# A decoder layer on one core: turns of attention weights placed only behind steps with products, and tokens sent to one expert a slot

## The chip, the cores and the metric

The kernel runs on one core of a Trainium2 chip. The metric is the device time of one execution in microseconds (us). The kernel before takes 1240.89 us, the median of 14 runs that lie between 1239.35 and 1242.22. The engines are named PE (TensorE, matrix products and transposes), DVE (VectorE), ACT (ScalarE), POOL (GpSimd) and SP (SyncE). Here POOL issues all indirect DMAs, which gather or scatter rows by a list of indices, and SP issues the plain ones.

## The reference

One layer on 32 batches of 112 tokens of width 256, all in 32-bit floats: self-attention of 16 heads with a causal window of 64, cross-attention of 16 heads on 375 context rows a batch with a relative bias, and a mixture of 8 experts (width 512), of which each token uses two. Cut to what matters:

```python
x = x + self_attention(layernorm(x))            # 16 heads, window 64
x = x + cross_attention(layernorm(x), context)  # 16 heads, 375 keys, bias by distance
xf = layernorm(x).reshape(3584, 256)
probs = softmax(xf @ router_w.T)                # 8 experts
probs = (probs * top2_mask) ; probs /= probs.sum(-1) + 1e-9
h = silu(xf @ gate_w[e] + gate_b[e]) * (xf @ up_w[e] + up_b[e])
x = x + sum over the two experts e of probs[e] * (h @ down_w[e] + down_b[e])
```

## The kernel before, in words

**Groups and slots.** The 32 batches form 8 groups (0 to 7) of 4 batches. The program is unrolled into *slots*. Group g owns the 16 slots from `base[g]` = 20 + 16g on; a slot takes a quarter of the cross-attention heads of one batch of that group, and a quarter of the self-attention heads of a batch two groups ahead. In slot s, `scores` (L464 ff.) lets PE make the raw scores (L477 cross, L488 self), DVE add bias or mask and take the row's minimum (L503), and POOL subtract that minimum from the whole tile (L509). Two slots later `weigh` turns the same tile: four PE transposes (L530) of up to 125 columns put one *turn* into a PSUM buffer, and one ACT activation (L531) empties it through exp. The pool of these PSUM buffers, `ps_tr`, has two. A slot with both kinds of scores has four turns (three of the cross scores, one, the *self turn*, of the self scores). `average` (L554) then multiplies the turned weights by the values; `divide` (L568 to L574, the last of them POOL's product into `by_q`), `turn` (L584, DVE) and `attended` (L597 on PE, L602 on DVE) finish a batch.

**Order.** The bodies of PE, DVE and ACT are issued exactly in the order in which the Python code calls them (`IN_ORDER`). The loop at the end of the program (L1266 ff.) does in each slot: the scores, the averages, the first two turns, then the list `steps[slot]` of other work with one of the remaining turns after each step, then whatever turns are left, then the list `late[slot]`, and a part of the planning or of the experts' tiles. Steps are put into the slots by hand with `put` and `put_late`: projections of keys and values for the coming batch (`cross_k`, L384; `cross_v`, L450), layer norms (`norm`, L344 to L353; `scale`, L364, which makes the tile `xn`; `norm_t`, L378, its transposes), the router, loads, and `blank`, which fills one of 28 parts of the DRAM table `xslots` with zeros and issues only a DMA on SP. POOL's instructions are put into the order of the program too (`queue_pool`); members of a *loose* group, such as "sent", may pass each other.

**Routing.** The functions of one route of a group are `logits` (L615), `choose` (L626 to L634), `rank` (L641 to L651, with POOL's product into `pr` at L643), `front`, `gate`, `weight_gates`, `count` and `address` (L718), each a slot after the one before. Then `send` writes each token's normalised row, its number and its gates (265 words) into two rows of `xslots`, one for each of its two experts (k = 0 and 1): an indirect DMA by POOL for each batch and each k (L725), eight for a group. The route of group g is sent in the slots after `base[g+1]`. The row tile of the third layer norm has the tag `xr`.

**Experts.** The experts work on tiles of up to 256 rows that have the same expert. `fetch_weights` (L960) gathers one expert's weights into the tile `w`, `fetch_rows` (L973) gathers two times 128 rows from `xslots` into `xg`; both are indirect DMAs on POOL. Tiles 0 and 1 are fetched while group 7 is still in attention, at `base[7]` + 5 to + 8. `experts` starts at `base[8]` + 5 and fetches tiles 2 and on, three tiles ahead. A tile is turned on PE (L1015, `xtp`), copied by DVE (L1020, `xT`), multiplied (L1030, `gu`), passed through silu on ACT (L1035) and DVE (L1038, `hid`), multiplied again (L1049, `py`), scaled by its gate on ACT (L1055, `y`) and added to the output in DRAM by an indirect DMA of POOL (L1056). For every `which == 0` tile, `fetch_rows` is told to follow the first 48 sends.

Of the kernel before, what the change touches and what calls it, by code (L numbers as in the profile page):

```python
# [11 lines left out]
F32 = mybir.dt.float32  # L12
# [7 lines left out]
B, S, D = 32, 112, 256  # L20
# [6 lines left out]
GB = 4  # L27
NG = B // GB
# [51 lines left out]
def decoder_kernel(  # L80
# [41 lines left out]
    def pool_order():  # L122


        traced = nc.cur_bb.bb.instructions
        mark, before_these, these, group = traced[-1], [], [], None

        def queue():
            nonlocal mark, before_these, these, group
            k = len(traced)  # L130
            while traced[k - 1] is not mark:
                k -= 1
            mark = traced[-1]
            for ins in traced[k:]:
                if ins.engine != mybir.EngineType.Pool:
                    continue
                own = loose.get(ins.name)
                if own is None or own != group:
                    before_these, these, group = these or before_these, [], own
                these.append(ins)  # L140
                for other in before_these:
                    tc.add_manual_dep(
                        ins, other.name,
                        mybir.DependencyInfo(
                            mybir.DependencyClass.NoSync, mybir.DependencyReason.DATA
                        ),
                        reason="order",
                    )

        return queue  # L150
# [25 lines left out]
    with ExitStack() as att, ExitStack() as own_att:  # L176
# [179 lines left out]
        def scale(g, n, b2):  # L356
            if b2 == 0:
                tag, width = ("xr", ROW) if n == 3 else ("xn", D)
                pool = keep if n == 3 else selfp
                xn = pool.tile([S, GB, width], F32, tag=tag, name=f"xn{g}_{n}")  # L360
                normed[g, n] = xn, *normed[g, n]
            xn, rstd, shift = normed[g, n]
            for b in (2 * b2, 2 * b2 + 1):
                nc.scalar.activation(  # L364
                    xn[:, b, :D], xs[g][:, b, :], AF.Identity,
                    bias=shift[:, b:b + 1], scale=rstd[:, b:b + 1],
                )
            if b2 == 1:
                normed[g, n] = [xn]
# [348 lines left out]
            nc.vector.tensor_copy(to, at)  # L718
            rows_of[g] = to

        def send(g, b):

            to, xn = rows_of[g], normed[g, 3][0]
            for k in range(2):
                sent = nc.gpsimd.indirect_dma_start(  # L725
                    out=xslots, out_offset=bass.IndirectOffsetOnAxis(
                        ap=to[:, k, b:b + 1], axis=0),
                    in_=xn[:, b, :], in_offset=None,
                )

                tc.declare_no_dep(sent.ins, group="sent", reason="rows differ")
                tc.add_to_no_dep_group("sent", sent.ins)
                all_sent.append(sent.ins)
                loose[sent.ins.name] = "sent"
# [343 lines left out]
        def experts():  # L1078


            fetch(2)
            pending, xT = None, begun[2]
            for k in range(body):
                if k + 3 <= body:
                    fetch(k + 3)
                if k:
                    hid = hidden_of(k)
                    for f in range(NFC):
                        hidden(k, xT, hid, f)
                        if f == 1:  # L1090
                            yield
                else:
                    hid = begun[1]
                    yield
                to, gate = target(k)
                yield
                if k:
                    xT = turned_in(k + 1)
                if pending is not None:
                    down(*pending)  # L1100
                pending = (k, hid, to, gate)
                if k == body - NTAIL:
                    left_over["n"] = nc.values_load(
                        in_tail[0:1, 0:1], min_val=0, max_val=NTAIL,
                        skip_runtime_bounds_check_because="at most so many are left",
                    )
            down(*pending)
            left_over["xT"] = xT
# [24 lines left out]
        def put(slot, fn, *args):  # L1133
            steps.setdefault(slot, []).append(partial(fn, *args))
# [4 lines left out]
        def put_late(slot, fn, *args):  # L1139
            late.setdefault(slot, []).append(partial(fn, *args))  # L1140

        def put_norm(norm_at, norm_t_at, g, n, scale_at=None):
            for c in range(NC2):
                put_late(norm_at - 2 + c, norm, g, n, c)
                put(scale_at or norm_at + 1, scale, g, n, c)
                put(norm_t_at, norm_t, g, n, c)
# [13 lines left out]
        def put_route(g, norm_at, norm_t_at):  # L1160
            put_norm(norm_at, norm_t_at, g, 3)
            put(norm_t_at + 1, logits, g)
            for i, fn in enumerate((choose, rank, front, gate, weight_gates, count, address)):
                put_late(norm_t_at + 1 + i, fn, g)
            for b in range(GB):
                put(norm_t_at + 8 + b, send, g, b)
            turn_at = 8 if g == NG - 2 else 7
            put(norm_t_at + turn_at, turn_gates, g)
            put(norm_t_at + (9 if g == NG - 1 else 10), down_bias, g)
# [60 lines left out]
        for g in range(NG):  # L1230
# [9 lines left out]
            if g >= NX:  # L1240
                put(base[g - NX + 1] + 22, load_x, g)
        put_route(NG - 1, base[NG] + 5, base[NG] + 8)
        free_self, free_all = base[NG - 1], base[NG] + 5
        plan_at = {base[EARLY + 1] - 1: first_plan, base[NG] + 14: later_plan}
# [9 lines left out]
        put(base[NG] + 4, begin_next)  # L1254
        put_late(base[NG] + 4, go_on, 3)

        made = {}
        with tc.manual_schedule(engines=IN_ORDER):
            queue_pool = pool_order()

            def do(part):
                part()
                queue_pool()

            planning, tiles = iter(()), iter(())
            for slot in range(min(steps), max(steps) + 1):  # L1266
                if slot == free_self:
                    own_att.close()
                    pool_of["early"] = ctx.enter_context(
                        tc.tile_pool(name="early", side="right", reuse_waits="tile")  # L1270
                    )
                if slot == free_all:
                    att.close()
                    for name, bufs in (("wts", 5), ("work", 3)):
                        pool_of[name] = ctx.enter_context(
                            tc.tile_pool(name=name, bufs=bufs, reuse_waits="tile")
                        )
                    tiles = experts()
                if slot in plan_at:
                    planning = plan_at[slot]()  # L1280
                if slot in items:
                    made[slot] = scores(*items[slot])
                parts = []
                if slot - 2 in items:
                    cross, selfs = items[slot - 2]
                    w = made.pop(slot - 2)
                    n = NKC * bool(cross) + len(selfs)
                    parts = [partial(weigh, cross, selfs, j, w) for j in range(n)]


                queue_pool()
                for half in range(2):
                    if sides := averages.get((slot, half)):
                        do(partial(average, half, sides.get("c"), sides.get("s")))
                for part in parts[:2]:
                    do(part)
                rest = parts[2:]
                for fn in steps.get(slot, []):
                    do(fn)
                    if rest:  # L1300
                        do(rest.pop(0))
                for part in rest:
                    do(part)
                for fn in late.get(slot, []):
                    do(fn)
                next(planning, None)
                next(tiles, None)
                queue_pool()
            for _ in planning:
                next(tiles, None)  # L1310
                queue_pool()
            for _ in tiles:
                queue_pool()
            queue_pool()
# [53 lines left out]
```

## Time and profile before

| quantity | value |
|---|---|
| median of 14 runs | 1240.89 us (1239.35 to 1242.22) |
| the profiled execution's own time | 1239.81 us |
| its span, first to last instruction | 1238.1 us |
| mean granted clock of PE over the span | 0.994 |
| subtraction of the minimum on POOL, L509 | 256 times, 1814 ns each |
| addition of bias or mask and minimum on DVE, L503, cross | 512 times, 542 ns |
| turns on ACT, L531 | 394 times, 542 ns |
| transposes of turns on PE, L530 | 1576 times, 275 ns |
| sends, L725 | 64 times, 966 ns, 2.6 us from issue to landing (median) |
| rows fetched, L973 | 60 times, 963 ns, 6.5 us to landing |

A row of the timeline gives the start and the duration in microseconds from the span's start, the engine, the line, the operation, the tiles written and read, and how many instructions stand together (x8 is two turns). Brackets at its end say how long the engine stood idle before it and what ended this: "<-ACT wT L531" means that it waited for ACT's instruction of line 531, "<-DMA" that a transfer had to land, "<-issue" that it waited for nothing that the profile shows.

### The profile page before, as it was taken

Reading aid. Unit: us, or ns where it says so; the run is one execution under the profiler, and the core shown is the slowest. Engines: PE = TensorE matmul, PEld = TensorE weight load, DVE = VectorE, ACT = ScalarE, POOL = GpSimd, SP = SyncE. Lnnn points to the kernel's source line nnn. Section 1 sums busy time; section 2 is a strip of 40 time slices with the busy share of each in tenths; the row PEclk is TensorE's granted clock in tenths of the full one; section 3 lists DMA queues with packets and bytes.
Section 4 is the critical chain, followed back from the end, with each engine's and each line's share of the span. In section 5 each row is a group of like instructions: output and inputs, shape, how many; then the busy total and the mean of one; then the engine's idle time right before and its main releaser. Section 6 shows DMA issues by size and latency. Waiting matters only on the chain. (4 is left out here: it accounts for less than half of the span.)

```text
span 1238.1 us, 29336 instructions
## 1 busy us (share of the span) xinstructions
PE 1205.5 (97%) x11522; PEld 955.3 (77%) x11522; DVE 644.1 (52%) x2989; ACT 563.8 (46%) x1186; POOL 828.2 (67%) x775
## 2 busy tenths in 40 slices
PE   9999999999999999999999999999899999999995
PEld 6666777777787778778778787777678888889885
DVE  4664555566656557566656666584525323223221
ACT  3454455556456546546555545535332223222221
POOL 7545665567777767776776778678766756555552
PEclk9999999999999999999999999999999999999998
DMA  8119887760200210020020011023177778887872
GB/s 230 39 26 221 182 187 171 159 146 14 74 15 15 55 45 15 21 67 15 26 60 15 14 46 41 14 72 121 46 252 207 191 199 258 246 246 217 247 200 26
DMA packets 69197, 137.48 MB, mean 111 GB/s; under 512 B 5377, under 2 KB 59970, under 8 KB 64450
## 3 DMA queue, kind: packets, MB, share of 16 engines
q0 software_dynamic: 19776, 80.39, 22.2%
q1 hardware_dynamic: 49282, 55.20, 18.8%
q8 instruction: 92, 1.51, 0.5%
q14 instruction: 47, 0.39, 0.1%
HBM read 85.74 MB, written 49.82 MB: 109 GB/s over the span
## 5 line engine op out<-in xcount | busy, mean ns | idle before, releaser
L509 POOL TENSOR_TENSOR w<-w,low 112x448 f32<-112x448 f32 (+1 forms) x256 | 459.4, 1814 | 204.6 <-DVE low L503 204.1
L503 DVE CUSTOM_DVE_ANT_0 w<-sc,bias 112x375 f32<-112x375 f32 x512 | 270.3, 542 | 123.9 <-PE sc L488 106.8
L531 ACT ACTIVATE wT<-wT 125x448 f32<-125x448 f32 (+1 forms) x394 | 198.5, 542 | 99.9 <-PE wT L530 93.5
L530 PEld LDWEIGHTS wT<-ident,w 112*125 112x125 f32 (+1 forms) x1576 | 187.6, 174 | 46.0 <-issue 14.5
L530 PE MATMUL wT<-ident,w 112*125 112x112 f32 (+1 forms) x1576 | 215.9, 275 | 5.7 <-ACT wT L531 5.7
L1030 PE MATMUL gu<-xT,w 128*128 128x256 f32 (+1 forms) x1152 | 216.3, 346 | 1.0 <-ACTq L1112 0.7
L1030 PEld LDWEIGHTS gu<-xT,w 128*128 128x128 f32 x1152 | 189.2, 191 | 24.8 <-issue 4.2
L1038 DVE SCALAR_TENSOR_TENSOR hid<-gu,w,sil 128x256 f32<-128x256 f32 (+1 forms) x144 | 62.9, 439 | 218.0 <-ACT sil L1035 214.9
L1056 POOL DMA_INDIRECT out_dram<-y,to x60 | 95.5, 1592 | 100.9 <-ACT y L1055 88.7
L503 DVE CUSTOM_DVE_ANT_0 w<-sc,wmask 112x112 f32<-112x112 f32 x512 | 129.0, 268 | 2.8 <-PE sc L488 2.8
L1035 ACT ACTIVATE sil<-gu,w 128x256 f32<-128x256 f32 (+1 forms) x144 | 62.9, 438 | 137.4 <-PE gu L1030 135.1
L477 PE MATMUL sc<-kT,q_cross 32*112 32x375 f32 x1024 | 122.7, 518 | 1.0 <-DVE low L503 1.0
L1049 PE MATMUL py<-w,hid 128*128 128x256 f32 x480 | 109.6, 380 | 0.4 <-DVE x L767 0.4
L1049 PEld LDWEIGHTS py<-w,hid 128*128 128x128 f32 x480 | 88.5, 190 | 11.4 <-DVE x L767 0.6
L450 PE MATMUL v2ps<-wkv_sb,ct 128*125 128x256 f32 x384 | 94.3, 381 | 0.0
L384 PE MATMUL k2ps<-ct,wkv_sb 128*128 128x375 f32 x256 | 92.6, 484 | 0.0
L503 DVE DVE_READ_ACCUMULATOR2_ANT low<- 112x1 f32 x1024 | 84.0, 82 | 0.0
L602 DVE TENSOR_TENSOR x<-x,ops 112x256 f32<-112x256 f32 x64 | 24.7, 418 | 106.3 <-PE ops L597 106.3
L725 POOL DMA_INDIRECT xslots<-xn,to x64 | 61.9, 966 | 19.1 <-issue 16.0
L450 PEld LDWEIGHTS v2ps<-wkv_sb,ct 128*125 128x125 f32 x384 | 67.2, 188 | 7.7 <-DVE q_cross L390 0.5
L1055 ACT ACTIVATE y<-py,gate 128x256 f32<-128x256 f32 x60 | 25.8, 471 | 103.5 <-PE py L1049 100.2
L973 POOL DMA_INDIRECT xg<-xslots,rows_i x60 | 57.8, 963 | 18.0 <-issue 16.8
(209 smaller groups left out, 1644.4 us busy)
## 6 DMA issues: line engine op xcount, KB each, us to landing
xslots<-zeros SPq DMA_DIRECT2D x28, 1060.0 KB, 8.4
ct<-in_ctx_t_dram SPq DMA_DIRECT2D x32, 375.0 KB, 3.6
x<-in_x_dram SPq DMA_DIRECT2D x8, 448.0 KB, 5.7
out_dram<-x SPq DMA_DIRECT2D x8, 448.0 KB, 4.2
bias<-by_rel_d SPq DMA_DIRECT2D x1, 2625.0 KB, 13.9
xslots<-xn,to POOLq DMA_INDIRECT x64, 2.6
xg<-xslots,rows_i POOLq DMA_INDIRECT x60, 6.5
out_dram<-y,to POOLq DMA_INDIRECT x60, 3.9
```

The source lines that it names most:

```text
L384: nc.tensor.matmul(ps, w[:, k, :], xT[:, k, :], start=(k == 0), stop=(k == NC2 - 1))
L450: nc.tensor.matmul(ps[:, i, :], ct[:, k, j * KC:(j + 1) * KC], wkv_sb[:, k, D:2 * D], start=(k == 0), stop=(k == NC2 - 1),)
L477: scored[cross] = nc.tensor.matmul(sc[r][:, :K], q[rows, p, b * S:(b + 1) * S], kT[rows, c, :], start=True, stop=True,).ins
L503: nc.vector.tensor_tensor_reduce(out=w[:, r, lo:hi], in0=sc[r][:, lo:hi], in1=add, scale=-1.0, scalar=FAR, op0=ALU.add, op1=ALU.min, accum ...
L509: nc.gpsimd.tensor_tensor(w[:, :, lo:hi], w[:, :, lo:hi], low[:, i].unsqueeze(2).to_broadcast([S, 4, hi - lo]), op=ALU.subtract,)
L530: nc.tensor.transpose(tp[:m, r, :], w[:, r, lo:lo + m], ident[:S, :S])
L531: nc.scalar.activation(wT[:m, j], tp[:m], AF.Exp, scale=-1.0)
L1030: nc.tensor.matmul(ps[:, m, :st], w[:, lo:lo + P], xT[:, c, :st], start=(c == 0), stop=(c == NC2 - 1),)
L1035: nc.scalar.activation(sil[:, :st], ps[:, 0, :st], AF.Silu, bias=w[:, bias_at + f:bias_at + f + 1])
L1038: nc.vector.scalar_tensor_tensor(hid[:, f, :st], ps[:, 1, :st], w[:, bias_at + NFC + f:bias_at + NFC + f + 1], sil[:, :st], op0=ALU.add, o ...
L1049: nc.tensor.matmul(py[:, h, :], hid[:, f, h * P:(h + 1) * P], w[:, lo:lo + D], start=(f == 0), stop=(f == NFC - 1),)
L1056: added = nc.gpsimd.indirect_dma_start(out=out, out_offset=row_of(to[:, h:h + 1]), in_=y[:, h, :], in_offset=None, compute_op=ALU.add,)
```

## The change

Three edits. The row tile `xr` of the third layer norm gets two buffers instead of one. In groups 0 to 6 `send` is called eight times, with one k each, in eight successive slots from `base[g+1]` + 1 on; before it was called four times, with both k, in four slots; the route of group 7 stays as it is. And a remaining turn is placed behind a step only if the step is not in the set `quiet`, whose members issue only DMAs or work for ACT (`load_x`, `load_context`, `blank`, `scale`, `send`, `fetch_weights`, `fetch_rows`).

```diff
@@ scale
-                xn = pool.tile([S, GB, width], F32, tag=tag, name=f"xn{g}_{n}")
+                xn = pool.tile(
+                    [S, GB, width], F32, tag=tag, name=f"xn{g}_{n}", bufs=2 if n == 3 else 1
+                )
@@ send
-        def send(g, b):
+        def send(g, b, ks=(0, 1)):
...
-            for k in range(2):
+            for k in ks:
@@ put_route
             for b in range(GB):
-                put(norm_t_at + 8 + b, send, g, b)
+                if g == NG - 1:
+                    put(norm_t_at + 8 + b, send, g, b)
+                else:
+
+                    for k in range(2):
+                        put(norm_t_at + 8 + 2 * b + k, send, g, b, (k,))
@@ the loop over slots
+        quiet = {load_x, load_context, blank, scale, send, fetch_weights, fetch_rows}
...
                 for fn in steps.get(slot, []):
                     do(fn)
-                    if rest:
+                    if rest and fn.func not in quiet:
                         do(rest.pop(0))
                 for part in rest:
                     do(part)
```

## The prediction

> **What bounds the kernel now.** I read the busy line first, then PE's timeline in three stages, then POOL's rows at the places where the change moves a DMA.
>
> ```profile
> PE 1205.5 (97%) x11522; PEld 955.3 (77%) x11522; DVE 644.1 (52%) x2989; ACT 563.8 (46%) x1186; POOL 828.2 (67%) x775
> ```
>
> PE is busy for 97% of the 1238.1 us span, so the time falls only where PE stops waiting, and rises only by waits that reach PE. A stretch in which groups 0 and 1 weigh their scores shows such a wait (start, us, engine, line):
>
> ```profile
> 148.61 1.12 PE L530 MATMUL wT<-ident,w 112*125 112x112 f32 x8
> 149.99 0.69 PE L530 MATMUL wT<-ident,w 112*125 112x112 f32 x4 [0.26 <-ACT wT L531]
> 150.52 1.44 PE L384 MATMUL k2ps<-ct,wkv_sb 128*128 128x375 f32 x4
> 151.80 0.55 PE L530 MATMUL wT<-ident,w 112*112 112x112 f32 x4
> ```
>
> Eight transposes are two turns. The third turn starts 1.38 us after them, since both PSUM buffers of the turns are full until ACT's exp (L531) has emptied one. A later slot has a product between:
>
> ```profile
> 408.18 1.12 PE L530 MATMUL wT<-ident,w 112*125 112x112 f32 x8
> 409.14 1.44 PE L384 MATMUL k2ps<-ct,wkv_sb 128*128 128x375 f32 x4
> 410.42 0.97 PE L530 MATMUL wT<-ident,w 112*125 112x112 f32 x8
> 411.23 0.93 PE L378 MATMUL tp<-ident,xn 112*128 112x112 f32 x8
> ```
>
> Here two turns take 0.96 us, not 1.38, and nothing waits: while PE multiplies for 1.28 us, ACT empties both buffers.
>
> **Part 1, the place of the turns.** The instruction order of the two built programs differs on PE in 26 slots (22 to 47), where the zero-fill step `blank` used to be followed by the third turn: turn, turn, turn, product becomes turn, turn, product, turn. Price of one: 1.38 - 0.96 = 0.42 us for the wait, and the third turn itself takes 150.52 - 149.99 = 0.53 us where half of the pair at 410.42 takes (411.23 - 410.42)/2 = 0.41; together 0.52 us (0.42 and 0.10, before rounding). Whole slots of equal make-up, with and without three turns in a row, take 7.69 and 7.17 us, 5.15 and 4.63, 5.47 and 4.93: again 0.52 to 0.54. 26 x 0.52 = **-13.5 us**. The lower bound is the idle time that the page itself puts down to L531 before L530, 5.7 us; I take 13.5, because start-to-start times carry it. What is late next: nothing that I see, as the product of 1.28 us covers two exps of 0.5 us. In 30 other slots only a short self turn changes its place behind or ahead of transposes; I price this at 0, bounded by 30 x 0.05 = 1.5 us to both sides.
>
> **Part 2, the sends.** A send takes 0.94 us on POOL and comes every 1.25. Number and order of DVE's and SP's instructions are unchanged; on POOL only sends move. In groups 2 to 6 eight sends now lie one in each of eight slots, not two in four. POOL idles 1.3 to 4.4 us ahead of its subtraction L509 there, and L509 ends at least 5.4 us before its turn: the cost is nothing, with 1.25 us a slot if that cover were gone. The second buffer of the tile `xr` keeps it alive until the eighth send; it costs no instruction.
>
> **Group 7** is different, since the first fetches of rows (L973) stand in the same slots as the later sends of group 5. They read what the sends write. Before, the sends are done; after, the built order is: send, rows x2, by_q, L509, send, weights, L509, send, rows x2. Rows wait for the send just issued, and that send for the rows before it. The rows of before at this place:
>
> ```profile
> 842.42 1.08 POOL L973 DMA_INDIRECT xg<-xslots,rows_i  x1 [0.17 <-issue]
> ...
> 843.81 0.96 POOL L973 DMA_INDIRECT xg<-xslots,rows_i  x1 [0.30 <-issue]
> ...
> 844.79 0.63 POOL L574 TENSOR_TENSOR by_q<-by_q,tot_av 128x256 f32<-128x256 f32 x1
> ...
> 845.46 0.45 DVE L584 STREAM_TRANSPOSE outs<-by_q 128x256 f32<-128x256 f32 x1 [5.23 <-POOL by_q L574]
> ...
> 845.96 1.12 PE L597 MATMUL ops<-wo_sb,outs 128*112 128x256 f32 x4
> ...
> 859.06 1.13 PE L530 MATMUL ctrwT<-ident,w 112*125 112x112 f32 x8
> ```
>
> In place of the rows at 842.42 stands a send. A quiet send lands 2.6 us after issue (the two at 832), 845.0 to 845.2 here, and POOL has resumed 0.75 us after a landing it waited for (961.21 after 960.46). So the rows begin at 845.9, and by_q at about 848.3, not 844.79: 3.5 us. DVE already waits 5.23 us for it at L584, the scores' adds stand behind L584 in DVE's fixed order, and PE's L597 follows within 0.5 us: PE +3.5. Then the send at +8 is issued at 856.8 and lands, behind the 1.6 MB of weights, at about 860.6 (sends among other transfers take 3.9 to 5.0); two rows, then L509, which ends near 866.4, while its turn (859.06 before, 862.6 with the first delay) wants it 3.85 us earlier. With 0.8 for by_q and pr behind it: **+8.2** (4, if only one wait counts, to 9).
>
> **The tail of the plan.** Group 6's sends were all ahead of the weights of tile 2. Now the order is: four sends, rstd, send, w2, rows x2, w3, rows x2, send, send, w4, rows x2, send, out adds. Each change between sending and reading `xslots` waits for a landing, and POOL carries out its DMAs in this order. The rows of before:
>
> ```profile
> 907.22 0.95 POOL L973 DMA_INDIRECT xg<-xslots,rows_i  x1 [0.30 <-issue]
> ...
> 914.72 1.66 POOL L1056 DMA_INDIRECT out_dram<-y,to  x1 [2.81 <-ACT y L1055]
> ...
> 922.15 0.25 POOL L643 TENSOR_TENSOR pr<-pr,tot 112x32 f32<-112x32 f32 x1
> 922.43 0.42 DVE L650 TENSOR_TENSOR gt<-pr 112x256 f32<-112x256 f32 x1 [3.65 <-POOL pr L643]
> ...
> 924.25 0.68 DVE L1020 COPY xT<-xtp 128x512 f32<-128x512 f32 x1
> ...
> 925.03 1.32 PE L1030 MATMUL gu<-xT,w 128*128 128x256 f32 x5 [0.30 <-issue]
> ```
>
> That such a change does wait, before shows once, for group 7's sends:
>
> ```profile
> 961.21 0.93 POOL L725 DMA_INDIRECT xslots<-xn,to  x1 [1.63 <-DMA xg<-xslots,rows_i]
> ```
>
> Rows land 2.9 us after issue with nothing beside them (843), 5.5 to 6.5 at 968 to 985, and here, among weights:
>
> ```profile
> DMA to landing us min/median/max: 7.1/8.0/8.7
> ```
>
> First wait: the rows of tile 2 wait for the fifth send, +1.95 us. The last rows of tile 3 are then issued at 907.22 + 1.95, about 909.15. With 6.5 us they land at 915.6, the second of the two sends behind them, which waits for them, goes at 916.35, w4 at 917.6, its rows at 918.9 and 920.1, landing at about 925.8, the last send at 926.5, the out add at 927.7 instead of 914.72: +12.9. pr is late by as much. DVE waits for it at L650 already, L1020 stands behind it, and PE's gu at 925.03 follows L1020 0.8 us later: PE **+12.9**. Bounds: all landings at 2.9 give 914.05 for w4's start, rows until 916.6, the out add at 921.5: +6.8; all at 8.7 give +18.4. I take 6.5, because fewer weights are in flight than at 907 once POOL waits.
>
> A page of the Trainium skill speaks against these two sums: "DMA: Bandwidth & Descriptors", section "Anatomy of one DMA — SWDGE (gpsimd) path", puts a transfer at about 2.0 us plus bytes over 436 KB/us. An estimate by it, 2.3 us for 119 KB sent or 136 KB fetched, agrees with 2.6 and 2.9 in the quiet rows, and is far from 7.1 to 8.7 at the tail. By the page alone, with 2.3 us in each wait, group 7 would cost 2 x (2.3 + 0.75) = 6.1 and the tail 5.3, and the change would end at about 1239.8, no change.
>
> **The clock.** PE's granted clock fell to 0.94 in 30 to 60 and 810 to 840 us, 1.8 us lost each, the second after PE had idled 0.68 us; longer idling may bring one more, +1 (0 to 3.6).
>
> **Sum**, against the profiled execution's 1239.81: -13.5 + 8.2 + 12.9 + 1 = +8.6, 1248.4. The median of 14 runs is 1.08 above that execution: **1249.5**. Its own range is 1243.5 (the tail at 6.8) to 1258 (the tail at 18.4 gives 1255, a gain of 5.7 in place of 13.5 gives 1257.3).
>
> **Rivals.** *The tail's waits are covered* (faster): pr may be late for nothing, if POOL passes the later sends or DVE's wait at L650 is absorbed. It decides at a tail delay under 13.5 - 8.2 = 5.3 us; with none, -13.5 + 8.2 + 1 = -4.3, 1236.6. For: DMA landings of 2.9 exist. Against: L650 waits 3.65 us now, and PE follows at once. *Neither wait reaches PE*: -13.5, 1227.4; against it stands the 5.23 at L584. *Half-priced waits*: quiet landings, 6.7 (two waits of 2.6 + 0.75) and 6.8 against 13.5, 1240.9. *The turns go on stalling* (the change does not do what it says), gain 0 to 5.7: 1257 to 1263; against it, the slots of equal make-up.
>
> **Chances.** Forecast 0.64, tail covered 0.13, neither 0.07, half-priced 0.10, stalls stay 0.06. 0.2% (2.5 us) is about what a measurement of this kernel can tell. Faster 0.20 (first two rivals), same 0.10, slower 0.70. The range 1234 to 1258 leaves out "neither", the far end of the forecast and "stalls stay", somewhat under 0.2.
>
> **What would show it.** In the changed kernel PE's third turns between 150 and 290 us should have no idle time before them; L973 and L725 should name a DMA as releaser near 840 to 865 and 900 to 930; DVE's wait at L584 should grow from 5.2 to 8.7 and at L650 from 3.7 to about 15; a third dip of the clock may stand there. I am wrong if POOL's DMAs wait less, or if DVE has other work to reach first.

## The result, and the profile after

The changed kernel takes 1256.26 us, the median of 6 runs (1255.63 to 1257.95), beside 1241.59 us for the kernel before, the median of 28 runs with those taken since. The ratio is 1.0126 with a 95% interval of 1.0115 to 1.0136: 15.6 us slower (14.7 by the two medians). The forecast was 1249.5, slower, with a range to 1258. The sign and the two large waits were right; the loss over the kernel before is nearly twice the 8.6 us that the sum gave. Its profiled execution took 1256.04 us, 16.2 more than that of before.

The changed kernel's page: busy time of the engines, and PE's granted clock in 40 slices of the span.

```profile
PE 1210.6 (97%) x11522; PEld 960.1 (77%) x11522; DVE 645.0 (51%) x2989; ACT 563.1 (45%) x1186; POOL 830.2 (66%) x775
...
PEclk9999999999999999999999999998989999999998
```

PE is as full as before, so the busy line does not show where the time went. Line numbers are two higher in the changed file from the third norm's tile on (L509 is now L511, L973 is L975).

What does show it is the start of the same PE row in both traces. The third column is the difference of the starts, taken before rounding, the fourth what each stretch adds to it.

| PE row, at (before) | at (changed) | difference | stretch adds | the forecast for it |
|---|---|---|---|---|
| first self scores, 15.93 | 15.29 | -0.64 | -0.64 | |
| averages, first slots of group 2, 296.11 | 282.94 | -13.16 | -12.53 | -13.5 |
| scores, group 7, 800.25 | 791.86 | -8.39 | +4.78 | 0 |
| scores, group 7, 823.54 | 814.44 | -9.10 | -0.72 | clock |
| output projection, 882.23 | 884.08 | +1.86 | +10.96 | +8.2 |
| down product, 912.69 | 916.24 | +3.55 | +1.69 | clock |
| gate product, 925.03 | 939.13 | +14.11 | +10.56 | +12.9 |
| gate product, 927.05 | 943.10 | +16.06 | +1.95 | clock |

Behind 927 the difference stays: 16.23 at 1225. The -0.72 is not the clock alone: a dip of before at 813 that is missing here gives about -1.6, and 0.9 comes back at the scores around 814, whose weight loads wait twice for DVE (0.20 us each).

**The turns.** The same work as the rows at 148.61 to 151.80 of before, now in the changed kernel's timeline of PE:

```profile
144.04 1.12 PE L532 MATMUL wT<-ident,w 112*125 112x112 f32 x8
145.00 1.44 PE L386 MATMUL k2ps<-ct,wkv_sb 128*128 128x375 f32 x4
146.28 0.97 PE L532 MATMUL wT<-ident,w 112*125 112x112 f32 x8
```

The product stands between, no row has idle time before it, and the pair takes 0.96 us where it took 1.38.

**Group 7.** The changed kernel's timeline there, POOL, DVE and PE:

```profile
837.48 0.99 POOL L975 DMA_INDIRECT xg<-xslots,rows_i  x1 [2.50 <-DMA xslots<-xn,to]
...
839.74 0.65 POOL L576 TENSOR_TENSOR by_q<-by_q,tot_av 128x256 f32<-128x256 f32 x1
...
840.42 0.45 DVE L586 STREAM_TRANSPOSE outs<-by_q 128x256 f32<-128x256 f32 x1 [8.98 <-POOL by_q L576]
...
840.92 1.97 PE L599 MATMUL ops<-wo_sb,outs 128*112 128x256 f32 x4 [3.87 <-DVE outs L586]
```

POOL waits 2.50 us for the send that it has just issued, DVE's wait has grown from 5.23 to 8.98, and PE stands idle 3.87 us before L599. The second wait of the same kind, some 15 us later:

```profile
853.49 0.96 POOL L975 DMA_INDIRECT xg<-xslots,rows_i  x1 [4.18 <-DMA xslots<-xn,to]
...
855.73 5.34 POOL L511 TENSOR_TENSOR w<-w,low 112x1500 f32<-112x1500 f32 x2
...
858.48 2.02 PE L532 MATMUL ctrwT<-ident,w 112*125 112x112 f32 x8 [3.57 <-POOL w L511]
```

4.18 us on POOL make the subtraction late, and PE's turn waits 3.57 us for it. Of the 10.96 us of this stretch the two waits of PE are 7.44.

**The tail of the plan**, in the changed kernel's timeline:

```profile
917.48 0.95 POOL L727 DMA_INDIRECT xslots<-xn,to  x1 [5.13 <-DMA xg<-xslots,rows_i]
...
927.56 0.96 POOL L727 DMA_INDIRECT xslots<-xn,to  x1 [5.34 <-issue]
...
928.83 1.66 POOL L1058 DMA_INDIRECT out_dram<-y,to  x1 [0.31 <-ACT y L1057]
...
936.25 0.25 POOL L645 TENSOR_TENSOR pr<-pr,tot 112x32 f32<-112x32 f32 x1
936.53 0.43 DVE L652 TENSOR_TENSOR gt<-pr 112x256 f32<-112x256 f32 x1 [14.21 <-POOL pr L645]
...
938.35 0.68 DVE L1022 COPY xT<-xtp 128x512 f32<-128x512 f32 x1
...
939.13 9.05 PE L1032 MATMUL gu<-xT,w 128*128 128x256 f32 x31 [10.86 <-issue]
```

The sends at 917.48 and 927.56 wait 5.1 and 5.3 us for the rows that were fetched before them; the second has no releaser named, but it stands where the order of POOL and the landing of the rows of tile 4 put it. The out add comes at 928.83 (927.7 in the forecast), DVE waits 14.21 us for pr (about 15), and PE 10.86 before its gate product.

**The clock.** PE's granted clock, the third figure from the right, in four stretches of the changed kernel:

```profile
839.00:845.00 6.00, 4.08 (x17) 2.10 (x18) 3.28 (x13) 0.00 (x0) 5.52 (x5) 0.72 0.21 57
857.00:865.00 8.00, 6.52 (x24) 5.59 (x28) 1.19 (x6) 1.88 (x4) 7.47 (x5) 0.57 0.00 1
911.00:915.00 4.00, 3.54 (x12) 2.82 (x13) 0.69 (x1) 0.00 (x0) 1.04 (x2) 0.71 0.92 347
938.00:943.00 5.00, 3.87 (x9) 3.18 (x10) 1.00 (x5) 0.08 (x1) 4.16 (x5) 0.50 0.58 172
```

In the trace's record the clock is at 0.5 for 3.4 us from 841.0, 6.8 from 858.1, 3.4 from 912.7 and 10.2 from 933.2. All four come with a wait of PE (3.87 us, 3.57, 1.93 for fetched rows before 911.45, and 10.86, in whose middle the last one starts): in the 3.4 us before each PE was busy for 0.08, 0.21, 1.46 and 0.00 us. In the first, L599 takes 1.97 us, not the 1.12 of before. Before had two dips of 3.4 us on the way to 925, at 52.1 and 813.3, after stretches in which PE was busy for 2.60 of 3.50 us and 2.95 of 3.40; the changed kernel has one like these at 90.1. So not every dip needs a long wait, and what brings these about is not shown.

### The profile page after: what moved, and what is told of

Same layout as the page of the kernel before. It is cut to its first block, busy times and chain, and to the rows that moved or that the text cites. A ratio compares the mean times of both kernels' runs of the same rounds, so it can differ in the third digit from the quotient of the medians.

```text
span 1254.2 us, 29314 instructions
## 1 busy us (share of the span) xinstructions
PE 1210.6 (97%) x11522; PEld 960.1 (77%) x11522; DVE 645.0 (51%) x2989; ACT 563.1 (45%) x1186; POOL 830.2 (66%) x775
## 5 line engine op out<-in xcount | busy, mean ns | idle before, releaser
L511 POOL TENSOR_TENSOR w<-w,low 112x448 f32<-112x448 f32 (+1 forms) x256 | 459.6, 1815 | 203.4 <-DVE low L505 201.7
L532 PEld LDWEIGHTS wT<-ident,w 112*125 112x125 f32 (+1 forms) x1576 | 190.7, 174 | 43.2 <-issue 19.0
L1051 PEld LDWEIGHTS py<-w,hid 128*128 128x128 f32 x480 | 89.6, 193 | 11.9 <-DVE x L769 0.6
L975 POOL DMA_INDIRECT xg<-xslots,rows_i x60 | 57.8, 963 | 24.7 <-issue 16.5
## 6 DMA issues: line engine op xcount, KB each, us to landing
bias<-by_rel_d SPq DMA_DIRECT2D x1, 2625.0 KB, 13.2
```

The source lines that it names most:

```text
L511: nc.gpsimd.tensor_tensor(w[:, :, lo:hi], w[:, :, lo:hi], low[:, i].unsqueeze(2).to_broadcast([S, 4, hi - lo]), op=ALU.subtract,)
L532: nc.tensor.transpose(tp[:m, r, :], w[:, r, lo:lo + m], ident[:S, :S])
L1051: nc.tensor.matmul(py[:, h, :], hid[:, f, h * P:(h + 1) * P], w[:, lo:lo + D], start=(f == 0), stop=(f == NFC - 1),)
```

## The experiments

They ran on two chips, 10 and 2 in the record: the scale step alone, the early groups alone, the kernel before for its trace, and the parts that gained on chip 2, the others on chip 10. On both the kernel before takes 1250 to 1255 us, 11 to 12 more than in the runs of the result. The record names no chip for these; "the first chip" below means theirs, "this chip" 10 or 2. Each kernel is compared with runs of before on its own chip; sums over experiments mix the two. Microseconds are worked out from the ratio and 1253.

**The zero-fill step alone.** The kernel before, with

```diff
+        quiet = {blank}
-                    if rest:
+                    if rest and fn.func not in quiet:
```

> The kernel before, with one edit: a turn is not placed behind the zero-fill step alone; the sends and the buffers stay. Theory (the third turn in a row waits for ACT, 0.52 us in each of 26 slots, and nothing else of the change gains): 13 us faster than before, 1227 to 1230 us. Rival (part of the gain in the first 300 us of the changed kernel is a dip of the clock that fell elsewhere, not the order): 5.7 to 9 us faster, 1232 to 1236.

Measured: 1241.03 us, ratio 0.9893 (0.9878 to 0.9908), 13.4 us faster. The theory holds: the whole gain of the turns is in this one step.

**The send alone as a quiet step.** The same with `quiet = {send}`.

> The kernel before, with one edit: a turn is not placed behind a send; sends and buffers stay as before. In the trace of the changed kernel PE falls back by 1.07 us in each of groups 2 to 6, at the slot of the down bias. Theory (the self turn now stands between the products of the down bias and the scores, which ran beside each other on PE before): 5 x 1.07 = 5.4 us slower than before, 1246 to 1248, with the same step in each of the five groups. Rival (the step is POOL's, from sends that lie in more slots): no change here, since the sends do not move, 1240 to 1243. The prediction priced the moved self turn at 0.

Measured: ratio 1.0040 (1.0027 to 1.0054), 5.0 us slower, with sends where they were. The rival falls. But the step was put too high: compared slot by slot on the first chip, the averages of the changed kernel start 13.16 us ahead of those of before at 308.4 and 12.51 at 322.8, so the down bias accounts for 0.66 us, in each of groups 2 to 5, and in the same way for 0.45 in group 6: 3.1 in all. They start 12.48 ahead at 374.9 and 12.09 at 387.0, about 0.4 from another slot, which comes four times: 1.7. Together this is the 4.8 of the table. In this run's own trace, beside before's of the experiments, the down bias costs 3.1 as well; another 1.3 lie just behind it in four groups, where PE itself starts its averages late (three idle times of 0.28 to 0.38 us from 322.5 to 324.3, with no releaser). So not all of the 5.0 us is the moved turn.

Before, around the down bias (PE):

```profile
319.96 0.97 PE L530 MATMUL wT<-ident,w 112*125 112x112 f32 x8
320.87 0.90 PE L762 MATMUL dbps<-db_sb,gT 32*112 32x256 f32 x6
321.40 0.57 PE L477 MATMUL sc<-kT,q_cross 32*112 32x375 f32 x2
321.60 0.38 PE L762 MATMUL dbps<-db_sb,gT 32*112 32x256 f32 x2
321.81 0.49 PE L477 MATMUL sc<-kT,q_cross 32*112 32x375 f32 x4
...
322.76 1.36 PE L554 MATMUL avc_s<-wT,v_cross 125*32 125x112 f32 x48
```

The changed kernel:

```profile
306.82 0.59 PE L532 MATMUL wT<-ident,w 112*125 112x112 f32 x4
307.34 1.43 PE L764 MATMUL dbps<-db_sb,gT 32*112 32x256 f32 x8
308.70 0.59 PE L532 MATMUL wT<-ident,w 112*112 112x112 f32 x4
309.23 0.90 PE L479 MATMUL sc<-kT,q_cross 32*112 32x375 f32 x8
...
310.25 0.97 PE L556 MATMUL avc_s<-wT,v_cross 125*32 125x112 f32 x32
```

Both kinds of product use 32 rows of PE (32*112). Before, scores start while the down bias still runs (321.40 lies ahead of 321.60), and from the turn to the averages it takes 322.76 - 319.96 = 2.80 us. With the self turn between, which uses 112 rows, the down bias runs out first: 310.25 - 306.82 = 3.43 us for the same work. That it is the rows, and not another property of the turn, is an argument; no run varies them.

**The scale step alone.** The same with `quiet = {scale}`.

> The kernel before, with one edit: a turn is not placed behind a scale step. Theory: in one slot of each of groups 2 to 6 the self turn's exp then stands behind four activations of the norm on ACT, not two, and PE's average waits for it, 0.4 us in the changed kernel's trace: 5 x 0.4 = 2 us slower. The prediction's price, and the rival (that step of 0.4 us has another cause): 0.

Measured: ratio 1.0017 (1.0007 to 1.0028), 2.1 us slower, as the theory had it; its trace beside before's on this chip shows four such steps of 0.40 us, not five. Before, ACT does half of the norm, the self turn's exp, and the other half, and PE's average follows without a wait:

```profile
374.06 1.09 ACT L364 ACTIVATE xn<-x,shift,rstd 112x256 f32<-112x256 f32 x2
375.04 0.54 ACT L531 ACTIVATE wT<-wT 112x448 f32<-112x448 f32 x1
375.46 1.09 ACT L364 ACTIVATE xn<-x,shift,rstd 112x256 f32<-112x256 f32 x2
...
376.04 0.57 PE L554 MATMUL avc_s<-wT,v_self 112*32 112x112 f32 x16
```

In the changed kernel both halves stand ahead of the exp, and PE's average, which reads it in the next slot, waits:

```profile
361.57 2.06 ACT L366 ACTIVATE xn<-x,shift,rstd 112x256 f32<-112x256 f32 x4
...
363.54 0.53 ACT L533 ACTIVATE wT<-wT 112x448 f32<-112x448 f32 x1
...
363.56 0.38 PE L556 MATMUL avc_s<-wT,v_self 112*32 112x112 f32 x8
364.12 0.40 PE L556 MATMUL avc_s<-wT,v_self 112*32 112x112 f32 x8 [0.19 <-ACT wT L533]
```

**The spread sends alone.** The changed kernel without `quiet` (`if rest:` as before).

> The changed kernel without its rule for the turns: only the sends are spread and the row tile has two buffers. Theory (fetches of rows and sends wait for one another in group 7 and behind the last slot, by the changed kernel's trace 10 to 11 us and 12 to 13 us, with 0 to 4 us of clock): 21 to 28 us slower than before, 1263 to 1270, and no step in groups 2 to 6. Rival (spread sends also take POOL's cover in groups 2 to 6): steps of about 1.07 us in the five groups, 5.4 us more.

Measured: ratio 1.0116 (1.0100 to 1.0131), 14.5 us slower: a miss of at least 6 us for the theory, and further from the rival. The next one but one says why.

**Groups 5 and 6 in pairs**, in the changed kernel:

```diff
-                if g == NG - 1:
+                if g >= NG - 3:
                     put(norm_t_at + 8 + b, send, g, b)
```

> The changed kernel, with the sends of groups 5 and 6 in pairs as before; groups 0 to 4 stay spread, the rule for the turns stays. Theory: both waits on landings are gone, 13 us gained by the turns and 5.4 lost behind the down bias stay, 1233 to 1236 us. Rival (the loss has another cause than the sends between the fetches, as a lower clock or the row tile's second buffer): still slower than before, 1245 to 1256.

Measured: 1242.29 us, ratio 0.9916 (0.9901 to 0.9932), 10.5 us faster than before. The bounds were written for the first chip's 1241; by their difference, 5.6 to 8.6 faster was expected. The loss does lie in the sends of these two groups. With the first three experiments above and the next one the parts sum to -13.4 + 5.0 + 2.1 - 5.6 = -11.9.

**Only the early groups spread.** The kernel just told, without `quiet`.

> The kernel before with the sends of groups 0 to 4 spread, one expert a slot, and two buffers of the row tile; groups 5 and 6 in pairs, no rule for the turns. The prediction: no cost and no gain, 0. Theory from the traces on this chip (the late copies of ACT shrink from 1.67 to 0.7 or 1.0 us when the sends are spread): 3 to 5 us faster than before.

Measured: ratio 0.9955 (0.9938 to 0.9971), 5.6 us faster. On the chips of the experiments the spread sends gain, where the forecast had nothing, and with 14.5 + 5.6 = 20.1 us the late groups cost what the theory lacked above, to within 1 us of its lower end.

**The kernel before, for its trace on this chip.**

> The kernel before, unaltered, for its trace on the chip of the experiments. Its time there is 1250 to 1255 us, 11 to 12 more than on the chip of the result. In the traces of the first two experiments, whose sends go in pairs, ACT's copy of the averages in the fourth slot of groups 2 to 6 starts about 2 us after its input is ready, without a releaser. Expected if this is the chip's doing: the same late copies here, 5 x 1.67 = 8.3 us, and the rest in the rows fetched behind the last slot. Rival (it comes from the edits): no late copy here.

Measured: 1253.31 us, one run. The late copies are there, in four groups and not five: the trace falls behind that of the first chip by 1.80, 1.64, 1.66 and 1.78 us. ACT and PE in the kernel before on this chip, fourth slot of group 2:

```profile
324.03 0.57 PE L554 MATMUL avc_s<-wT,v_self 112*32 112x112 f32 x16
...
326.97 0.53 ACT L558 COPY outs<-avc_s 128x448 f32<-128x448 f32 x1 [5.25 <-PE v2ps L450]
```

The averages end at 324.6 and the copy starts 2.4 us later. With the early sends spread (the last experiment below) the averages end at 312.46 and the copy starts 0.7 us later:

```profile
311.84 0.62 PE L556 MATMUL avc_s<-wT,v_self 112*32 112x112 f32 x16
...
313.18 0.53 ACT L560 COPY outs<-avc_s 128x448 f32<-128x448 f32 x1 [3.64 <-PE wT L532]
```

What ACT waits for is not in the traces. In both, a store of 448 KB, sends and one packet of the instruction queue fall into these 2 us; that an instruction of ACT comes late behind them is an argument, not shown. On the first chip the same store, two sends and one such packet fall into 322 to 327 us of before, and the copy starts 0.1 us after the averages end (324.59), so these transfers alone do not make it late. With the send as a quiet step it is PE that starts late at this place, not ACT.

**Group 6 alone in pairs** (`if g >= NG - 2`), in the changed kernel.

> The changed kernel, with the sends of group 6 alone in pairs as before, so that none stands between the fetches of tiles 2, 3 and 4; group 5's stay spread. Theory: the wait behind the last slot is gone (12 to 15 us with the clock's dip behind it), the one in group 7 stays: 12 to 15 us faster than the changed kernel on the same chip. Rival (the two waits hide one another, or the time comes back in the tail): under 6 us faster.

Measured: 1251.33 us, 9.3 less than the changed kernel's 1260.65 on this chip. It is less than the 12 to 15 expected and well over the rival's 6.

**Group 5 alone in pairs** (`if g in (NG - 1, NG - 3)`), in the changed kernel.

> The changed kernel, with the sends of group 5 alone in pairs as before, so that the fetches of tiles 0 and 1 in group 7 find all sends landed; group 6's stay spread. Theory: the wait in group 7 is gone, 9 to 11 us faster than the changed kernel on the same chip. Rival (what group 7 loses is made up later, since POOL has idle time there): under 4 us faster.

Measured: 1253.30 us, 7.4 less than the changed kernel: between the two, nearer to the theory's 9. Both waits together, 16.7, agree with the 18.4 that the pair of them gave back above (1260.65 - 1242.29).

**The send taken out of the quiet steps**, in the changed kernel.

> The changed kernel, with the send alone taken out of the steps behind which no turn is placed; the down bias then has its scores next to it again. Theory: 5 x 1.07 = 5.4 us faster than the changed kernel on the same chip, and no step in groups 2 to 6 against before. Rival (the step in these groups came from the spread sends): same as the changed kernel within 1.5 us.

Measured: 1255.70 us, 5.0 less than the changed kernel. The step at the down bias is gone from the trace; the 0.4 us of the scale step stays. Beside the trace of the changed kernel on this chip (the next run), 3.1 us come back at the down bias and 2.1 just behind it, where this chip has its late instructions.

**The changed kernel once more.**

> The changed kernel once more, unaltered, beside the three others on one chip, so that they can be compared with it. Expected: 13 to 16 us slower than before, as it was, if the chip does not matter; the chip of the first four experiments gave 11 to 12 us more to the kernel before, and there the sum of the parts (13.4 gained, 5.0 and 14.0 lost) would be 6 us slower.

Measured: ratio 1.0074 (1.0052 to 1.0096), 9.3 us slower than before: between the two figures. On the way from group 2 to 6 its trace falls behind that of the first chip by 1.0 us in each of four groups, the kernel before by 1.7, which accounts for 2.8 of the 6.3 us between the two losses; the rest is open. So the loss of 15.6 us is that of one chip; that it is a loss holds on this one too.

**The parts that gained.** `quiet = {blank}` and `if g >= NG - 3`, two buffers of the row tile.

> The parts that gained, together: a turn is not placed behind the zero-fill step (no other step is excepted), groups 0 to 4 send one expert a slot, groups 5 and 6 in pairs as before. Theory: 13.4 us from the turns and 3 to 5 from the spread sends on this chip, 16 to 19 us faster than before, and faster than the kernel with the zero-fill edit alone. Rival (the spread sends bring nothing beside the turns): 13 to 14 us faster.

Measured: 1235.09 us, ratio 0.9854 (0.9836 to 0.9872), 18.3 us faster than before, beside 13.4 + 5.6 = 19.0 from its parts. It beats both kernels. On the first chip, where the late copies of ACT are not seen, it was not run.

## Why the prediction was right, and where it was not

- **The turns: right.** -13.5 forecast, -12.5 in the stretch, -13.4 alone on the other chip. The page's own idle time, 5.7 us, would have been less than half: the start-to-start times were the row to take.
- **Sends against fetches: right.** Group 7 was forecast at 8.2 with waits of 3.5 and 3.85; PE waited 3.87 and 3.57. The rest of the 10.96 us, 3.5, is put down to the clock: its two dips there last 10.2 us at 0.5, an estimated 5.1 us of work at most. The tail was forecast at 12.9: the out add comes 14.1 us later than before (928.83 for 914.72), and 1.7 of these were there when POOL began rstd (900.00 for 898.32), which leaves 12.4. PE lost 1.69 to the clock before it reached its wait, so 10.56 was left to wait; together 12.25. That 12.9 lies so close is partly luck: with its own 6.5 us for both landings the steps of the prediction add up to 14.0, and 12.9 comes from 5.7 us for the second. Measured were 6.9 and 5.5 us (rows issued at 910.13 and 921.27), and the first wait added 1.25 us, not 1.95.
- **The moved self turns: wrong, and the largest miss.** "I price this at 0, bounded by 30 x 0.05 = 1.5 us to both sides" was 4.8 us by the two traces of the first chip (3.1 at the down bias and 1.7 behind the scale step). I counted what a short turn takes, and not what it parts on PE, nor what is then ahead of its exp on ACT. Both neighbours could be read in the trace of before.
- **The clock: mis-sized.** +1 forecast; 3.5 in group 7 and 1.95 behind the tail's wait, less 1.6 for the dip at 813 that went, are about 3.9. Dips come with PE's long waits, as argued, and one for all of them was too few.
- **A rule that spoke against it.** The rows fetched between the sends of the tail took 5.4 to 7.8 us to land, 6.4 in the middle; the 6.5 taken from rows of before was right. By the Trainium skill, "DMA: Bandwidth & Descriptors", section "Anatomy of one DMA — SWDGE (gpsimd) path", they would have taken an estimated 2.3 us; where the two differ, the measurement decides.
- **The early sends: right on the first chip**, where the two steps above make up the 4.78 us of groups 2 to 6 and leave nothing for the sends, and not on chip 2, where spreading them gains 5.6.

Of the 7.5 us between the 8.6 of the sum and the 16.1 of the table, 4.8 lie in groups 2 to 6, where the sum had nothing, and 2.8 in group 7, where the clock was sized too small; the first 296 us (-13.2 for -13.5) and the tail with the clock's other stretches (13.5 for 13.9) are right to within 0.4. The measured 1256.3 us lies inside the range, but not for what set the range's upper end, a tail of 18.4 us or a gain of 5.7 from the turns: that it holds is partly luck.

## What to carry to other kernels

A rule that passes over a step which only issues a transfer can still part two pieces of work that ran well side by side: when a scheduling rule moves an instruction, read both its new neighbours on its engine, and what is now ahead of its consumer. Before transfers are spread out, look for readers of the same memory in the slots that they move into: each change between writing and reading waits for one landing, and all that the queue's engine has to do waits with it. A rule that helps one kind of step (here the zero-fill) is best tried on that kind alone.

## What the runs showed of the hardware

The products of the down bias and of the scores, which use 32 rows of PE each, overlap when they are neighbours in the order: eight of the down bias and the slot's sixteen scores take 1.89 us together (320.87 to 322.76), and 1.36 and 1.02 us when a turn of 112 rows parts them (307.34 to 308.70, 309.23 to 310.25). The kernel before took 1241.6 us in the runs of the result and 1252.6 to 1253.2 on chips 10 and 2; 7 of these 11 to 12 us are one late copy of ACT in each of four groups, of which the trace names no cause.
